# A binary-weight layer behind a two-way decaying scan: where the last batch's bias and x are added

## The chip, the cores and the metric

The kernel runs on one core of one Trainium2 chip. The metric is the time of one launch on the device in microseconds (us); lower is better. Engines go by the profile's names beside their own: PE is TensorE, DVE is VectorE, ACT is ScalarE, POOL is GpSimd, SP is SyncE, which only issues transfers here.

## The reference, cut to what matters

```python
def _bi_wkv(r, k, v, w, u, time_emb):          # r = x; k = v = fside; time_emb = cond
    tf = sigmoid(sum(time_emb, axis=-1))[:, None, None]
    decay = exp(-exp(w))[None, :] * (0.5 + 0.5 * tf[:, :, 0])
    ek = exp(minimum(k, 30.0)); ekv = ek * v
    # forward and backward scans over the tokens: a = a * decay + ekv_t, b = b * decay + ek_t
    nf, df = scan(ekv, ek); nb, db = scan(ekv, ek, reverse=True)
    euk = exp(minimum(u + k, 30.0))
    num = nf + nb - ekv + euk * v
    den = df + db - ek + euk
    return sigmoid(r) * (num / maximum(den, 1e-08)) * (0.8 + 0.2 * tf)

def binarize_weight(w):
    alpha = mean(abs(w), axis=1, keepdims=True)
    return where(w >= 0, 1.0, -1.0) * alpha

out = x + einsum('bsi,oi->bso', _bi_wkv(x, fside, fside, w, u, cond), binarize_weight(weight)) + bias
```

`x`, `fside` and `out` are [4, 1024, 1024] float32 (batch, token, channel), `weight` is [1024, 1024], `bias` is [1024].

## The kernel before, in words

Channels lie on partitions and tokens along the free dimension. The 4 batches of 8 channel blocks (128 channels, all 1024 tokens) make 32 steps, `for g in range(steps)`. The order of all instructions is written out by hand (`tc.manual_schedule()`); each engine works through its own list, and engines and transfers wait for each other by semaphores.

A step works at several blocks at once. SP loads block g + 2 of fside (`load_k`, tile `k_rows`) and of x (`load_gate`, tile `sg_rows`) and, in the first eight steps, 128 rows of the weight (`load_weight`, L237). TensorE transposes them. ScalarE takes the exponentials of the next block. VectorE runs the four scans of block g, forward (L366) and backward (L379), for `num` and for `den`. The backward scan begins from a value that ScalarE computes in `act_edge` (L372; `edge_num`, `edge_den`). For block g - 1, VectorE adds the own term to the denominator (`dve_denominator`, L389), and GpSimd issues a transfer that adds the own term `euk` into `num` (`dma_own_numerator`, L384). Then comes the division: GpSimd's `floor_den` (L396), ScalarE's logarithm (`act_log`, L404) and exponential (`act_reciprocal`, L411), GpSimd's `den_product` (L416) and `num_product` (L419), VectorE's gate with the sigmoid of x (`dve_newton_gate`, L423), GpSimd's `gated_product` (L428). For block g - 2 the result is split into two parts for TensorE, by ScalarE (`act_hi`, L433) and GpSimd (`lo_part`, L438). In steps 1 to 8 ScalarE also prepares the weight (`prepare_weight`, L247 and L254).

For batches 0 to 2 the product with the weight has output channels on partitions. ScalarE scales it and adds the bias (`act_scale`), TensorE turns it back, ScalarE copies it to a staging tile and SP stores it to `out`. Then x is added by an accumulating transfer from DRAM to DRAM, 256 rows (1 MB) at a time: `add_x` (L140), issued by GpSimd. The table `adds` gives the step for each; entry 32 means after the loop. In a step that has one, the logarithm is placed behind `act_edge` instead of ahead of it:

```python
            if g > 0 and not adds[g]:
                act_log(g - 1)
            ...
            act_edge(g, nums[g], "edge_num")
            if g > 0 and adds[g]:
                act_log(g - 1)
```

The last batch goes another way, with tokens on partitions, so that no turning back is needed. Its 8 groups of 128 tokens, in two halves of 512 channels each, are the "wide" products (`pe_wide_product`, L517). `leave_wide` (L534, L536) multiplies a sum in PSUM by `alpha_rows` and adds it to `x_rows[n]`, the 128 rows of x that `load_x_rows` (L479) has loaded. Group 6 (`begun`) is computed in two portions: its first five channel blocks in step 30, copied by ScalarE to `partials[0]`; its last three at the very end, in three pieces named `rest`. Products of groups 0 to 3 wait for the last two channel blocks; those of 4, 5 and 7 are done whole behind them. The `po` and `kT` PSUM buffers rotate among these sums. Before the change the bias of the last batch is loaded along rows into `bias_rows` (L496) and added to each `x_rows[n]` by `add_bias` (L831): by GpSimd for group 6, which also joins its partial sum there (L839, L840), by VectorE for the seven others. SP stores the rows (`store_rows`, L834).

Of the kernel before, what the change touches and what calls it, by code (L numbers as in the profile page):

```python
# [21 lines left out]
def kernel(  # L22
# [27 lines left out]
    nc = tc.nc  # L50
    P = 128
    B, T, C = x.shape
    TD = time_emb.shape[1]
    NT = T // P
    NC = C // P
# [6 lines left out]
    rows = ctx.enter_context(tc.tile_pool(name="rows", bufs=2))  # L62
# [3 lines left out]
    eu_pool = ctx.enter_context(tc.tile_pool(name="eu_pool", bufs=3))  # L66
# [47 lines left out]
    def group(q):  # L114
        b, r = divmod(q, NH * NC)
        h, oc = divmod(r, NC)
        return b, h, oc


    def pair_of(t, q):  # L120
        b, h, oc = group(q)
        return t[b, h * H : (h + 1) * H, oc * P : (oc + 2) * P].rearrange(
            "(n p) c -> p n c", p=P
        )
# [8 lines left out]

    def store(q):
        nc.sync.dma_start(out=pair_of(out, q), in_=x_pairs[q])

    def add_x(b, n):

        rows = slice(2 * n * P, 2 * (n + 1) * P)
        nc.gpsimd.dma_start(  # L140
            out=out[b, rows, :], in_=x[b, rows, :], accum_op=ALU.add, max_dma_last_dim=8192
        )
# [92 lines left out]
    def load_weight(oc):  # L235
        wr = resid.tile([P, C], F32, tag="x_res", name=f"w_rows_{oc}")
        nc.sync.dma_start(out=wr, in_=weight[oc * P : (oc + 1) * P, :])  # L237
        w_rows[oc] = wr
# [235 lines left out]
    x_rows = {}  # L474
    last = B - 1

    def load_x_rows(n, pool, tag):
        t = pool.tile([P, C], F32, tag=tag, name=f"x_rows_{n}")
        nc.sync.dma_start(out=t, in_=x[last, n * P : (n + 1) * P, :])  # L479
        x_rows[n] = t  # L480


# [11 lines left out]
    def load_along_rows(pool, tag, name, values):  # L494
        t = pool.tile([P, C], F32, tag=tag, name=name)
        nc.sync.dma_start(out=t, in_=values.unsqueeze(0).to_broadcast([P, C]))  # L496
        return t
# [35 lines left out]
    def leave_columns(ps, n, cols):  # L533
        nc.vector.tensor_mul(ps, ps, alpha_rows[:, cols])  # L534
        xs = x_rows[n][:, cols]
        nc.vector.tensor_add(xs, xs, ps)  # L536

    def leave_wide(n, part):
        leave_columns(wide[n, part], n, columns(part))


    begun = NT - 2
    partial_ps = {}
    partials = []
# [18 lines left out]
    steps = B * NC  # L563
# [25 lines left out]
    q, g = groups, 2 * NC  # L589
# [3 lines left out]
    q, g = 2 * groups, 3 * NC  # L593
# [6 lines left out]
    fill(g + 2, 0, pieces(range(q + 5, q + groups)))  # L600

    adds = {g: [] for g in range(steps + 1)}
    for b in range(B - 1):
        for n in range(NT // 2):
            adds[min((b + 2) * NC + 2 * n - 2, steps)].append((b, n))

# [5 lines left out]
    g = 3 * NC  # L616
# [3 lines left out]
    with tc.manual_schedule():  # L620
# [3 lines left out]
        for i, v in enumerate((u, bias)):  # L624
            nc.gpsimd.dma_start(
                out=ub_rows[i * NC : (i + 1) * NC, :],
                in_=v.rearrange("(n c) -> n c", c=P),
# [50 lines left out]
        for g in range(steps):  # L678
            b, cc = divmod(g, NC)
            final = g == steps - 1  # L680
            if g + 2 < steps:
                load_k(g + 2)
                for i in gate_loads[g]:
                    load_gate(i)
            else:
                load_x_rows(g + 2 - steps, rows, "k_rows")
                load_x_rows(g + 4 - steps, gate_rows, "sg_rows")
            if g < NC:
                load_weight(g)
            if final:  # L690
                alpha_rows = load_along_rows(den_pool, "den", "alpha_rows", alpha_dram)

            if g > 0:
                dve_denominator(g - 1)
                dma_own_numerator(g - 1)
            for i in adds[g]:
                add_x(*i)
            if final:
                done()
            scale()  # L700
            if final:
                act_partial(1)
            done()
            if g > 1:
                act_hi(g - 2, 0)
                act_hi(g - 2, 1)
            product(parts[g][0])
            if final:
                pe_wide_product(1, 1, range(NC - 3))
                pe_wide_product(2, 0, range(NC - 3))  # L710
            turn()
            if g > 0:
                floor_den(g - 1)
            if g > 0 and not adds[g]:
                act_log(g - 1)
            pool_clamp(g)
            if g > 1:
                lo_part(g - 2, 0)
                lo_part(g - 2, 1)
            product(late[g][:2])  # L720
            if late[g]:
                done()
            if g > 0:
                forward(g, nums[g])
# [3 lines that stand above are left out]
            if g > 0:  # L728
                act_reciprocal(g - 1)
                den_product(g - 1)  # L730
            if g > 0:
                dve_own_terms(g)
            scale()
            done()
            leave()
            if 1 <= g <= NC:
                prepare_weight(g - 1)
            if g == NC:
                out_scales()
            if not final:  # L740
                pe_transpose_k(g + 1)
                product(late[g][2:])
                act_exponentials(g + 1)
                act_own_exponentials(g + 1)
            scale()
            product(parts[g][1])
            turn()
            if final:
                for i in ((1, 0), (1, 1), (2, 0)):
                    pe_wide_product(*i, range(NC - 3, NC - 2))  # L750
                pe_wide_product(0, 0, range(NC - 2))
            backward(g, nums[g], "edge_num")
            if final:
                dma_own_numerator(g)
            if g > 0:
                num_product(g - 1)
            forward(g, dens[g])
            act_edge(g, dens[g], "edge_den")
            leave()
            done()  # L760
            scale()
            product(parts[g][2])
            if g == steps - 2:
                pe_partial(0)
            if g > 0:
                dve_newton_gate(g - 1)
            if g > 0 and not final:
                gated_product(g - 1)
            for i in gates[g]:
                act_gate(i)  # L770
            if gates[g]:
                log_exp_tables()
            pe_transpose_gate(g)
            if g == 3 * NC - 1:
                load_gate(g + 4)
            product(parts[g][3])
            turn()
            if g == steps - 2:
                leave()
                act_partial(0)  # L780
                pe_partial(1)
            if parts[g][4]:
                done()
            product(parts[g][4])
            if g == steps - 2:
                pe_wide_product(1, 0, range(NC - 3))
            leave()
            backward(g, dens[g], "edge_den")
            if not final:
                dve_numerator_terms(g + 1)  # L790
            if g == NC:
                store_alpha()
# [3 lines left out]
        g = steps - 1  # L796
# [27 lines left out]
            lo_part(g, h, nc.vector)  # L824
        for n in (5, 7):
            load_x_rows(n, eu_pool, "eu")

        bias_rows = load_along_rows(eu_pool, "eu", "bias_rows", bias)

        def add_bias(n, engine=nc.vector):  # L830
            engine.tensor_add(x_rows[n], x_rows[n], bias_rows)  # L831

        def store_rows(n, cols=slice(0, C)):
            nc.sync.dma_start(  # L834
                out=out[last, n * P : (n + 1) * P, cols], in_=x_rows[n][:, cols]
            )

        add_bias(begun, nc.gpsimd)
        nc.gpsimd.tensor_mul(partials[0], partials[0], alpha_rows)  # L839
        nc.gpsimd.tensor_add(x_rows[begun], x_rows[begun], partials[0])  # L840
        waiting = [(n, part) for n in range(4) for part in range(2)]
        for i in waiting:
            pe_wide_product(*i, range(NC - 2, NC))
        for i in waiting:
            leave_wide(*i)
        for n, part, biased in (
            (4, 0, (0,)), (4, 1, (1, 4)), (5, 0, (2, 3)), (5, 1, (5,)), (7, 0, (7,)), (7, 1, ())
        ):
            pe_wide_product(n, part, range(NC))

            for i in ((0, 1) if part else ()) if n == 5 else (part,):
                leave_wide(n, i)
            for i in biased:
                add_bias(i)
                if i != 7:
                    store_rows(i)
        store_rows(7)
        for cols in (slice(0, H), slice(H, 3 * H // 2), slice(3 * H // 2, C)):
            t = ps_o.tile([P, cols.stop - cols.start], F32, tag="po", name=f"rest_{cols.start}")
# [33 lines left out]
```

## Time and profile before

| what | value |
|---|---|
| device time, median of 3 runs | 489.73 us (489.09 to 491.17) |
| profiled execution | 489.64 us, span 487.9 us |
| mean granted TensorE clock | 0.898 |
| busy: VectorE, GpSimd, TensorE, ScalarE | 98%, 84%, 75%, 69% of the span |
| HBM read, written | 55.59 MB, 29.36 MB |
| the 12 `add_x` transfers | 1024 KB each, median 11.9 us from issue to landing |

The span runs from the first to the last instruction of the profiled execution; the rest of the device time lies around it. A line such as "start, us, engine line op out<-in" is one instruction or a run of like ones; brackets show the idle time of the engine ahead of it and what ended it. A landing is the time from a transfer's issue to its completion.

### The profile page before, as it was taken

To read this page: it belongs to the slowest core of one execution; us is meant where nothing else is said; L and a number is where in the kernel's file an instruction comes from. 1 tells how busy PE (TensorE), PEld (TensorE's weight loads), DVE (VectorE), ACT (ScalarE), POOL (GpSimd) and SP (SyncE) were. 2 spreads that over 40 slices of the span, in tenths; PEclk is the share of its full clock that TensorE was granted. 3 is DMA by queue.
4 is the path that set the end of the run, shared out by engine and by line. 5 is a ranking of instruction groups with operands and counts; after the bars stand their busy time and mean duration, and the time that the engine had idled before them with its cause. 6 is when DMAs were issued, how large, how long until landed. Compare 5 with 4: busy or idle time off the path is not lost.

```text
span 487.9 us, 5199 instructions
## 1 busy us (share of the span) xinstructions
PE 363.6 (75%) x1803; PEld 295.7 (61%) x1803; DVE 477.0 (98%) x330; ACT 337.3 (69%) x468; POOL 410.7 (84%) x279
## 2 busy tenths in 40 slices
PE   3434433344588877778899998965999998999995
PEld 2333332233466666656777777754887777887884
DVE  6999999999999999999999999999999999998997
ACT  4795968869595967869697879787866979734000
POOL 3379999999999999999999999999999999991240
PEclk9975566666699999999999999985999999999998
DMA  8865565556465555959787996889559697899743
GB/s 228 246 172 144 159 165 142 142 133 149 107 152 150 144 143 137 233 143 248 184 201 164 259 234 166 185 200 230 130 100 273 156 265 220 186 266 267 166 198 145
DMA packets 89761, 89.48 MB, mean 183 GB/s; under 512 B 2660, under 2 KB 80776, under 8 KB 88200
## 3 DMA queue, kind: packets, MB, share of 16 engines
q1 hardware_dynamic: 83320, 59.78, 40.9%
q0 software_dynamic: 6400, 29.37, 31.3%
q8 instruction: 14, 0.23, 0.2%
q14 instruction: 11, 0.09, 0.1%
q10 hardware_dynamic: 16, 0.00, 0.0%
HBM read 55.59 MB, written 29.36 MB: 174 GB/s over the span
## 4 chain that ended last, share of the span: by engine, by line
DVE 78%; PE 13%; issue 4%; ACT 3%; POOL 1%; DMA 0%; SPq 0%; DVEq 0%; ACTq 0%
DVE num L379 13%; DVE den L379 13%; DVE num L366 12%; DVE den L366 12%; DVE den L389 6%; DVE num L350 6%; DVE den L423 6%; PE wide L517 5%; DVE euk L356 3%; PE po L449 3%; DVE x_rows L831 2%; DVE x_rows L536 1%; DVE wide L534 1%; PE partial L517 1%; PE bank L517 1%
## 5 line engine op out<-in xcount | busy, mean ns | idle before, releaser
L449 PE MATMUL po<-gated,wT 128*128 128x512 f32 x768 | 199.4, 408 | 0.3 <-ACT staged L559 0.3
L449 PEld LDWEIGHTS po<-gated,wT 128*128 128x128 f32 x768 | 141.5, 192 | 30.5 <-ACT staged L559 0.7
L266 PE MATMUL kT<-ident,k_rows 128*128 128x128 f32 x248 | 42.1, 325 | 62.1 <-issue 43.2
L272 PE MATMUL sgT<-ident,sg_rows 128*128 128x128 f32 x256 | 43.2, 323 | 46.7 <-DVE den L423 41.4
L438 POOL TENSOR_TENSOR gated<-num,gated 128x512 fp32r<-128x512 f32 x60 | 75.8, 1283 | 2.4
L266 PEld LDWEIGHTS kT<-ident,k_rows 128*128 128x128 f32 x248 | 33.8, 167 | 69.7 <-issue 51.7
L379 DVE TENSOR_TENSOR_SCAN den<-bank,edge_den,den 128x1024 f32<-128x1024 f32 x32 | 74.8, 2338 | 0.4 <-ACT edge_den L372 0.4
L416 POOL TENSOR_TENSOR den<-den,eu 128x1024 f32<-128x1024 f32 x31 | 73.9, 2385 | 1.4 <-ACT eu L411 1.4
L379 DVE TENSOR_TENSOR_SCAN num<-bank,edge_num,num 128x1024 f32<-128x1024 f32 x32 | 74.8, 2336 | 0.0
L419 POOL TENSOR_TENSOR num<-num,eu 128x1024 f32<-128x1024 f32 x31 | 73.8, 2380 | 0.5 <-DMA num<-euk 0.5
L428 POOL TENSOR_TENSOR num<-den,num 128x1024 f32<-128x1024 f32 x30 | 71.8, 2394 | 2.8 <-DVE den L423 0.5
L366 DVE TENSOR_TENSOR_SCAN den<-bank,den 128x1024 f32<-128x1024 f32 x32 | 72.2, 2256 | 0.0
L366 DVE TENSOR_TENSOR_SCAN num<-bank,num 128x1024 f32<-128x1024 f32 x31 | 70.6, 2276 | 0.0
L272 PEld LDWEIGHTS sgT<-ident,sg_rows 128*128 128x128 f32 x256 | 35.0, 166 | 57.5 <-DVE den L423 30.2
L433 ACT CAST gated<-num 128x512 fp32r<-128x512 f32 x64 | 36.5, 619 | 28.6 <-POOL num L428 24.8
L396 POOL TENSOR_SCALAR den<-den,floor 128x1024 f32<-128x1024 f32 x31 | 37.1, 1196 | 19.8 <-DVE den L389 15.7
L404 ACT ACTIVATE eu<-den,gain 128x1024 f32<-128x1024 f32 (+1 forms) x33 | 36.9, 1121 | 24.3 <-POOL den L396 19.4
L517 PE MATMUL wide<-wT,gated 128*128 128x512 f32 x192 | 45.1, 392 | 0.0
L559 ACT COPY staged<-turned 128x512 f32<-128x512 f32 x48 | 27.5, 574 | 21.2 <-PE turned L469 21.2
L389 DVE SCALAR_TENSOR_TENSOR den<-eu,top,den 128x1024 f32<-128x1024 f32 (+1 forms) x33 | 41.5, 1259 | 0.0
L517 PEld LDWEIGHTS wide<-wT,gated 128*128 128x128 f32 x192 | 35.9, 188 | 8.2 <-ACT gate_of_last L810 0.4
L356 DVE SCALAR_TENSOR_TENSOR euk<-eu,top,kT 128x1024 f32<-128x1024 f32 x31 | 38.7, 1249 | 0.0
(100 smaller groups left out, 589.4 us busy)
## 6 DMA issues: line engine op xcount, KB each, us to landing
sg_rows<-in_x_dram SPq DMA_DIRECT2D x32, 512.0 KB, 6.3
num<-euk POOLq DMA_DIRECT2D x32, 512.0 KB, 5.8
k_rows<-in_fside_BxSxS_dram SPq DMA_DIRECT2D x31, 512.0 KB, 4.9
out_dram<-staged SPq DMA_DIRECT2D x24, 512.0 KB, 5.7
out_dram<-in_x_dram POOLq DMA_DIRECT2D x12, 1024.0 KB, 11.9
w_rows<-in_L_ffn_weight_dram SPq DMA_DIRECT2D x8, 512.0 KB, 5.9
x_rows<-in_x_dram SPq DMA_DIRECT2D x8, 512.0 KB, 7.7
out_dram<-x_rows SPq DMA_DIRECT2D x7, 512.0 KB, 2.6
```

The costliest lines, as they stand in the source:

```text
L266: nc.tensor.transpose(kT[:, s * P : (s + 1) * P], k_rows[g][:, s, :], ident)
L272: nc.tensor.transpose(t[:, s * P : (s + 1) * P], sg_rows[g][:, s, :], ident)
L356: nc.vector.scalar_tensor_tensor(euk, eus[g], top[:, b, cc : cc + 1], k_ps[g], ALU.min, ALU.mult)
L366: nc.vector.tensor_tensor_scan(t, decay_row(g), t, 0.0, ALU.mult, ALU.add)
L379: nc.vector.tensor_tensor_scan(back, decay_row(g), back, inits[g, which], ALU.mult, ALU.add)
L389: nc.vector.scalar_tensor_tensor(dens[g][:, ts], eus[g][:, ts], top[:, b, cc : cc + 1], dens[g][:, ts], ALU.min, ALU.add,)
L416: engine.tensor_mul(dens[g][:, ts], dens[g][:, ts], eus[g][:, ts])
L419: engine.tensor_mul(nums[g][:, ts], nums[g][:, ts], eus[g][:, ts])
L428: engine.tensor_mul(nums[g][:, ts], dens[g][:, ts], nums[g][:, ts])
L438: engine.tensor_sub(t[:, 1, :], nums[g][:, h * H : (h + 1) * H], t[:, 0, :].bitcast(F32))
L449: nc.tensor.matmul(prods[q], wT[:, cc, oc * P : (oc + 1) * P], gated[b, cc, h][:, i, :], start=(cc == 0 and i == 0), stop=(cc == NC - 1 an ...
L517: nc.tensor.matmul(t, gated[last, cc, h][:, i, s * P : (s + 1) * P], wT[:, cc, cols], start=(cc == ends[0] and i == 0), stop=(cc == ends[1 ...
```

## The change

Three things are changed. Rows of the last batch in `out` are filled with the bias by four transfers from SP (steps 2, 5, 7, 9; the bias row repeated 256 times), and x is added onto them by four `add_x` transfers from GpSimd (steps 6, 10, 12, 14). `load_x_rows` then reads `out` instead of x, so that x and bias arrive together. The `add_x` of the other batches move two steps later: those of batch 0 to steps 16 to 22, of batch 1 to 24 to 30, all four of batch 2 behind the loop, where three were before. At the end `bias_rows` and all `add_bias` go; VectorE joins group 6's partial sum behind the sums of group 4, in place of GpSimd; and rows are stored as soon as both their halves are done.

```diff
+    def begin_rows(n):
+        rows = slice(2 * n * P, 2 * (n + 1) * P)
+        nc.sync.dma_start(
+            out=out[B - 1, rows, :], in_=bias.unsqueeze(0).to_broadcast([2 * P, C])
+        )
...
     def load_x_rows(n, pool, tag):
         t = pool.tile([P, C], F32, tag=tag, name=f"x_rows_{n}")
-        nc.sync.dma_start(out=t, in_=x[last, n * P : (n + 1) * P, :])
+        nc.sync.dma_start(out=t, in_=out[last, n * P : (n + 1) * P, :])
...
     for b in range(B - 1):
         for n in range(NT // 2):
-            adds[min((b + 2) * NC + 2 * n - 2, steps)].append((b, n))
+            adds[min((b + 2) * NC + 2 * n, steps)].append((b, n))
+
+    begins = {g: n for n, g in enumerate((2, 5, 7, 9))}
+    for n, g in enumerate((6, 10, 12, 14)):
+        adds[g].append((last, n))
...
             if g < NC:
                 load_weight(g)
+            if g in begins:
+                begin_rows(begins[g])
...
-        bias_rows = load_along_rows(eu_pool, "eu", "bias_rows", bias)
-
-        def add_bias(n, engine=nc.vector):
-            engine.tensor_add(x_rows[n], x_rows[n], bias_rows)
...
-        add_bias(begun, nc.gpsimd)
-        nc.gpsimd.tensor_mul(partials[0], partials[0], alpha_rows)
-        nc.gpsimd.tensor_add(x_rows[begun], x_rows[begun], partials[0])
         waiting = [(n, part) for n in range(4) for part in range(2)]
         for i in waiting:
             pe_wide_product(*i, range(NC - 2, NC))
-        for i in waiting:
-            leave_wide(*i)
-        for n, part, biased in (
-            (4, 0, (0,)), (4, 1, (1, 4)), (5, 0, (2, 3)), (5, 1, (5,)), (7, 0, (7,)), (7, 1, ())
-        ):
+        for n, part in waiting:
+            leave_wide(n, part)
+            if part == 1:
+                store_rows(n)
+        for n, part in ((4, 0), (4, 1), (5, 0), (5, 1), (7, 0), (7, 1)):
             pe_wide_product(n, part, range(NC))
 
             for i in ((0, 1) if part else ()) if n == 5 else (part,):
                 leave_wide(n, i)
-            for i in biased:
-                add_bias(i)
-                if i != 7:
-                    store_rows(i)
+            if (n, part) == (4, 1):
+                nc.vector.tensor_mul(partials[0], partials[0], alpha_rows)
+                nc.vector.tensor_add(x_rows[begun], x_rows[begun], partials[0])
+            if part == 1 and n != 7:
+                store_rows(n)
         store_rows(7)
```

## The prediction, made before the result

> **What bounds the kernel now.** I read the page's busy times and its chain first.
>
> ```profile
> PE 363.6 (75%) x1803; PEld 295.7 (61%) x1803; DVE 477.0 (98%) x330; ACT 337.3 (69%) x468; POOL 410.7 (84%) x279
> ...
> DVE 78%; PE 13%; issue 4%; ACT 3%; POOL 1%; DMA 0%; SPq 0%; DVEq 0%; ACTq 0%
> ```
>
> VectorE is busy almost all the time and carries the chain: 32 steps of 13.5 us. But 98% is an average, and what the change takes off VectorE lies in the last 37 us only. So I read the timeline of that stretch.
>
> ```profile
> 454.78 23.97 PE L517 MATMUL wide<-wT,gated 128*128 128x512 f32 x104
> ...
> 463.56 3.23 DVE L831 TENSOR_TENSOR x_rows<-x_rows,bias_rows 128x1024 f32<-128x1024 f32 x1
> ...
> 478.59 2.24 PE L517 MATMUL rest<-wT,gated 128*128 128x512 f32 x12
> ...
> 480.11 0.69 DVE L534 TENSOR_TENSOR wide<-wide,alpha_rows 128x512 f32<-128x512 f32 x1
> ```
>
> The columns are start, length, engine, line. To be seen: TensorE runs 104 wide products without a break to about 478.75, and VectorE takes the last sum, (7, 1), at 480.11. VectorE is only 1.4 us behind TensorE there, whatever it did before.
>
> **The end, term by term.** VectorE loses seven `add_bias`. By the starts of the instructions behind them they take 3.15 (463.56 to 466.71) + 5.44 (four from 468.04 to 473.48) + 1.14 + 1.15 = 10.9 us. It gains two operations of the same size and kind (1.15 each) for the partial sum: 2.3 us. Net 8.6 us less work. How much of it counts is set by TensorE, whose instructions stay the same, in the same order. I lay the new VectorE list against the product times (16 matmuls of 0.230 us each, 23.97/104; the first eight of the 104 finish group 3). The eight waiting sums leave from 451.3 to 462.2 as now. The products of group 4 end at about 460.3 and 464.0, and their sums (1.33 us each) leave by 465.4. The partial sum follows to 467.7. Group 5 leaves after its second product (471.4) by 474.1, (7, 0), done at 475.1, by 476.4, and (7, 1) starts when its product ends at 478.75, not at 480.11. Ahead of each of these VectorE idles, 0.5 + 3.7 + 1.0 + 2.3 = 7.5 us in all. Behind (7, 1) lie the same sums as now, 4.4 us to 484.5. The third `rest` product waits for (7, 1)'s PSUM buffer as now, moved by as much, and ends about 0.6 us before VectorE asks for it. I allow 0.1 us for the hand-over: **-1.2 us**, bounds -1.4 (all of the lag) and 0. The stores behind it (3.4 us from 484.5 to the end of the span) are the same, and the others only leave earlier.
>
> GpSimd's three operations at the end (8.1 us), behind the bias load, ended by 469.1, before the path needed them: taking them out gives nothing. A fourth x transfer is issued at the end instead of three. The three issued from 438.2 landed after at most 21.7 us, by about 461; four at the same pace end by 468, and nothing waits for them but the program's end: nothing.
>
> **The loop: three more x transfers** (steps 6, 10, 12; the one in step 14 and those up to 30 take places that transfers of other batches have now). GpSimd queues the issue between the own-term transfer (L384) and `floor_den` (L396), whose chain runs over ScalarE's logarithm to `den_product` (L416) and VectorE's gate, L423. A step without one, a step with one, and the only stall:
>
> ```profile
> 88.75 1.11 POOL L396 TENSOR_SCALAR den<-den,floor 128x1024 f32<-128x1024 f32 x1 [0.78 <-DVE den L389]
> ...
> 195.88 1.14 POOL L140 DMA_DIRECT2D out_dram<-in_x_dram  x1
> 196.79 1.40 POOL L396 TENSOR_SCALAR den<-den,floor 128x1024 f32<-128x1024 f32 x1
> ...
> 258.71 1.22 DVE L423 SCALAR_TENSOR_TENSOR den<-den,sgT 128x1024 f32<-128x1024 f32 x1 [0.15 <-POOL den L416]
> ```
>
> The 0.78 us gap takes the issue in. What is left is VectorE's L389 of the step after, 1.33 us at 208.83 where 1.27 is usual, and one stall of 0.15 among the nine transfers in the loop now. Three more: 3 x 0.06 + 0.15 = **+0.3 us**, bounds 0 and 3 x 0.2. The issue also waits for its fill, which left SP four steps or more before: nothing.
>
> The Trainium skill (SBUF — State Buffer, "Who interferes with whom") says that a VectorE instruction with two SBUF inputs and a GpSimd instruction that reads SBUF lock each other out for the whole instruction. The first `add_bias`, 3.23 us beside GpSimd's product against 1.23 alone, agrees; what the lock would make of the three transfers goes into the third rival.
>
> **Step 6 has a cost that the diff hides.** In a step with a transfer the code puts the logarithm (L404, now at 89.89) behind `act_edge` (90.95 to 91.23). Steps 10 and 12 look like 14, where this stalls nobody. In step 6 ScalarE also prepares weights:
>
> ```profile
> 91.13 1.14 ACT L411 ACTIVATE eu<-eu,ln_g 128x1024 f32<-128x1024 f32 x1
> ...
> 96.40 0.29 ACT L372 ACTIVATE edge_den<-den,edge 128x1 f32<-128x1 f32 x1
> 97.41 2.33 DVE L379 TENSOR_TENSOR_SCAN den<-bank,edge_den,den 128x1024 f32<-128x1024 f32 x1
> ```
>
> Between 91.13 and 96.40 ScalarE has no gap. The logarithm (1.17 us to the next start in step 14) moves in at 91.13, so `edge_den` starts at about 97.6 and ends at 97.9, and the scan waits 0.5 us: **+0.5 us**, bounds 0.3 and 0.7.
>
> **The fills**, four of 1 MB on SP's queue behind a step's loads (steps 2, 5, 7, 9). No row shows a copy of this kind. The nearest, with the us from issue to landing last:
>
> ```profile
> num<-euk POOLq DMA_DIRECT2D x32, 512.0 KB, 5.8
> ...
> out_dram<-x_rows SPq DMA_DIRECT2D x7, 512.0 KB, 2.6
> ...
> bias_rows<-in_L_ffn_bias_dram SPq DMA_DIRECT2D x1, 512.0 KB, 13.1
> ```
>
> Twice 2.6 us to twice 13.1 us (the same repeated row, but read while three x transfers ran): 5 to 26 us; I take 8, near the first, since the DMA engines are only half busy there (share 0.59 in 67.5 to 81 and in 94.5 to 108). What is queued behind on SP comes a step later: k rows issued at 80.50 are first transposed some 25 us after and land in 4.9; gate rows wait 18 us for their sigmoid and land in 6.3. Even 26 us fits, so SP's queue costs nothing, nor do the x loads that now read `out`, whose transfers ended long before. What could show is the sharing of engines with `num<-euk`: issued at 87.10, read by GpSimd at 95.84, 8.7 us of room against 5.8. **0 us**; the upper bound is the second rival.
>
> The Trainium skill (DMA: Bandwidth & Descriptors, "Anatomy of one DMA") puts a transfer at about 2.0 us plus bytes over 436 GB/s, an estimate of 4.4 us for one fill; by that the sum is the same, and no run shows one yet.
>
> **Sum.** The profiled execution took 489.64 us (span 487.9 and 1.7 around it), 0.09 under the median of 489.73. 489.64 - 1.2 + 0.3 + 0.5 + 0 = 489.2, as a median 489.3. That is a change of 0.1%. A measurement of this kernel can tell about 0.5%, 2.4 us, from no change.
>
> **Rivals.** First: VectorE's work comes off whole, 489.3 - 8.6 + 1.2 = 481.9. For it: VectorE has hardly a gap from 451 to 484. Against: TensorE's unbroken row to 478.75, which would have to end before 471. Chance 0.04.
>
> Second, slower: the fills of steps 2, 5 and 7 hold back the `num<-euk` beside them. It decides once that lands more than 8.7 us after its issue; GpSimd then starts `num_product` late, has 0.8 us of gap to catch up, and VectorE's gate in the next step waits. At the longest 512 KB landing of the queue rows above, 13.1, each costs 13.1 - 8.7 - 0.8 = 3.6 us, three 11: 500. For it: GpSimd waits 0.5 us for this transfer once already. Against: its landings stay under 9.8 even beside x transfers and stores. Chance 0.08, most of it at 492 to 496.
>
> Third, slower: each new x transfer pushes a GpSimd instruction onto a VectorE one with two SBUF inputs, and VectorE is shut out for 2.0 us, as in the 3.23 us row: 489.3 + 3 x 2.0 = 495.3. Against: the nine transfers in the loop show 0.06 to 0.21. Chance 0.03.
>
> That the change doesn't do what it says I leave out: in the new order of instructions VectorE has seven additions fewer and two operations more, and nothing else of it moves.
>
> **How the numbers follow.** The forecast has 0.85. Its bounds are 488.3 (-1.4, nothing given back) and 491.1 (no gain, +1.3), nearly all within 0.5%. Faster gets the first rival and 0.01 of the forecast's edge, 0.05; slower the other two and 0.02 of it, 0.13; 0.82 stays the same. I stretch the range to 487.8 and 491.9 for the scatter of single runs (489.09 to 491.17 shown); it leaves out the rivals, 0.15.
>
> **What would show it.** In the new profile: (7, 1)'s sum starting at about 478.8 plus what the loop gave back, with idle time on VectorE put down to PE wide; step 6's scan waiting about 0.5 us for ACT `edge_den`; L389 at 1.33 after steps 6, 10 and 12; `num<-euk` still landing in about 6 us and the fills in about 8. It is wrong if VectorE shows no idle time behind TensorE at the end, or if GpSimd waits for `num<-euk`.

## The result and the profile after

The changed kernel took 488.21 us (median of 20 runs, 487.97 to 489.95), the kernel before 489.33 us on the same chip (20 runs, 488.14 to 491.22): a ratio of 0.9975, interval 0.9965 to 0.9984. That is 1.1 us less: the interval leaves out 1, so the gain is real, but it lies within the 0.5% that the prediction called no change. It is also 1.1 us under the forecast of 489.3, and 0.1 us under the 488.3 that the prediction's terms gave as their lower bound; it falls into the range of 487.8 to 491.9, which was stretched for the scatter of single runs. The profiled execution took 488.17 us, its span 486.4 us.

The page's busy times and its chain, as shown of before:

```profile
PE 364.9 (75%) x1803; PEld 297.1 (61%) x1803; DVE 468.9 (96%) x325; ACT 337.4 (69%) x468; POOL 406.2 (84%) x280
...
DVE 76%; PE 17%; issue 3%; ACT 3%; DMA 0%; SPq 0%; DVEq 0%; ACTq 0%
```

VectorE lost 8.1 us of work, and the time 1.5 us. TensorE's share of the chain rose from 13% to 17%: what VectorE no longer does at the end it spends waiting. The timeline of the end (start, length, engine, line; L523 was L517, L540 was L534) shows where:

```profile
454.84 23.97 PE L523 MATMUL wide<-wT,gated 128*128 128x512 f32 x104
...
464.20 0.70 DVE L540 TENSOR_TENSOR wide<-wide,alpha_rows 128x512 f32<-128x512 f32 x1 [0.49 <-PE wide L523]
...
471.52 0.70 DVE L540 TENSOR_TENSOR wide<-wide,alpha_rows 128x512 f32<-128x512 f32 x1 [3.50 <-PE wide L523]
...
475.19 0.70 DVE L540 TENSOR_TENSOR wide<-wide,alpha_rows 128x512 f32<-128x512 f32 x1 [0.79 <-PE wide L523]
...
478.85 0.70 DVE L540 TENSOR_TENSOR wide<-wide,alpha_rows 128x512 f32<-128x512 f32 x1 [2.25 <-PE wide L523]
```

The 104 products take the same 23.97 us, and VectorE now stands idle ahead of four sums, 0.49 + 3.50 + 0.79 + 2.25 = 7.0 us, each time for TensorE. (7, 1) starts at 478.85, right behind its product.

In the loop, take a step's length as the time from the start of the backward `den` scan of the step before to that of its own. From the first to the last of these scans the loop takes 419.66 us, against 419.52 before. It gives back 0.23 at step 6 (13.73 against 13.50) and 0.06 behind each of steps 10 and 12, and gains 0.20 at step 18 (13.55 against 13.75), which the prediction did not have. Step 6:

```profile
90.92 1.13 ACT L410 ACTIVATE eu<-den,gain 128x1024 f32<-128x1024 f32 x1
...
97.22 0.30 ACT L378 ACTIVATE edge_den<-den,edge 128x1 f32<-128x1 f32 x1
97.56 2.35 DVE L385 TENSOR_TENSOR_SCAN den<-bank,edge_den,den 128x1024 f32<-128x1024 f32 x1
```

The scan waits for ScalarE's `edge_den` as foretold, but for 0.2 us, not 0.5. Step 18 is read from three lines. The first is the x transfer's issue on GpSimd in before (L140). The second is the landing of the store that SP issued ahead of it, at 245.89. The third is the x transfer's issue after the change (L146).

```profile
250.54 0.86 POOL L140 DMA_DIRECT2D out_dram<-in_x_dram  x1 [0.22 <-issue]
```

```profile
out_dram<-staged SPq DMA_DIRECT2D x1, 512.0 KB, 4.0
```

```profile
250.30 1.16 POOL L146 DMA_DIRECT2D out_dram<-in_x_dram  x1
```

In before this transfer adds x to rows 512 to 767 of batch 0, and the last store to these rows is that one: issued at 245.89 with a landing of 4.0 us, it lets GpSimd start at 250.54. The row itself names no releaser for the 0.22 us; that it is the store is read from these times and borne out in experiment 1. With the x transfers two steps later, no store of the same rows is under way, and the wait is gone.

The queue rows of the two new kinds of transfer, and the landing of the `num<-euk` issued at 100.67, beside the third fill:

```profile
out_dram<-in_x_dram POOLq DMA_DIRECT2D x16, 1024.0 KB, 11.7
out_dram<-in_L_ffn_bias_dram SPq DMA_DIRECT2D x4, 1024.0 KB, 10.1
...
num<-euk POOLq DMA_DIRECT2D x1, 512.0 KB, 8.6
```

A fill lands in 10.1 us at the median. Beside the first three fills the `num<-euk` land in 7.8, 7.8 and 8.6 us, where the same three took 4.5 to 4.6 before. The point from which the prediction's second rival would decide was 8.7.

### The profile page after: what moved, and what is told of

It reads as the page before. It is cut to its first block, busy times and chain, and to the rows that moved or that the text cites. A ratio compares the mean times of both kernels' runs of the same rounds, so it can differ in the third digit from the quotient of the medians.

```text
span 486.4 us, 5204 instructions
## 1 busy us (share of the span) xinstructions
PE 364.9 (75%) x1803; PEld 297.1 (61%) x1803; DVE 468.9 (96%) x325; ACT 337.4 (69%) x468; POOL 406.2 (84%) x280
## 4 chain that ended last, share of the span: by engine, by line
DVE 76%; PE 17%; issue 3%; ACT 3%; DMA 0%; SPq 0%; DVEq 0%; ACTq 0%
DVE den L385 13%; DVE num L385 13%; DVE num L372 13%; DVE den L372 12%; PE wide L523 9%; DVE den L395 7%; DVE num L356 6%; DVE den L429 6%; DVE euk L362 3%; PE po L455 3%; PE partial L523 1%; PE wide_t L523 1%; PE bank L523 1%; PE sgT L278 1%; PE kT L272 1%
## 5 line engine op out<-in xcount | busy, mean ns | idle before, releaser
L523 PE MATMUL wide<-wT,gated 128*128 128x512 f32 x192 | 45.1, 392 | 0.0
L523 PEld LDWEIGHTS wide<-wT,gated 128*128 128x128 f32 x192 | 35.9, 188 | 8.2 <-ACT gate_of_last L821 0.4
## 6 DMA issues: line engine op xcount, KB each, us to landing
out_dram<-in_x_dram POOLq DMA_DIRECT2D x16, 1024.0 KB, 11.7
out_dram<-in_L_ffn_bias_dram SPq DMA_DIRECT2D x4, 1024.0 KB, 10.1
```

What stands on the lines that cost most here:

```text
L523: nc.tensor.matmul(t, gated[last, cc, h][:, i, s * P : (s + 1) * P], wT[:, cc, cols], start=(cc == ends[0] and i == 0), stop=(cc == ends[1 ...
```

## The experiments

Unless said otherwise, times are medians, and ratios are against the kernel before on the same chip with 95% intervals. Three groups of runs were made, with the kernel before at 489.79, 489.72 and 489.80 us.

**1. Which part does what.** Four kernels of the first group do parts of the change alone. The tail only (x is loaded as before, there are no fills, and the bias of the last batch is left out), as a diff against the changed kernel:

```diff
-        nc.sync.dma_start(out=t, in_=out[last, n * P : (n + 1) * P, :])
+        nc.sync.dma_start(out=t, in_=x[last, n * P : (n + 1) * P, :])
...
-            adds[min((b + 2) * NC + 2 * n, steps)].append((b, n))
-
-    begins = {g: n for n, g in enumerate((2, 5, 7, 9))}
-    for n, g in enumerate((6, 10, 12, 14)):
-        adds[g].append((last, n))
+            adds[min((b + 2) * NC + 2 * n - 2, steps)].append((b, n))
...
-            if g in begins:
-                begin_rows(begins[g])
```

> The end of the changed kernel alone: the loop, its x transfers and the x loads are those of the kernel before, there are no fills, and the last batch's bias is left out. Theory (TensorE's last products set the end as soon as VectorE has no backlog): -1.3 us against before, VectorE idle some 7 us at the end. Rival A (VectorE's removed work counts whole): -8.6 us. Rival B (the gain comes from the x transfers being two steps later): 0.

Measured: 487.67 us (12 runs), 0.9961 [0.9944, 0.9977]. The interval, 1.1 to 2.7 us less, leaves out both rivals, 8.6 and 0. The medians are 2.1 us apart, more than the lag of 1.4 us that the prediction saw at the end. Between the two profiled executions (487.61 and 489.64) the time from the start of the first wide sum to the end of the last gives 1.34 us of the difference, what follows the last sum 0.58 (2.80 against 3.38) and the start of the loop 0.19; why the last two are shorter was not tried.

The fills, the four new x transfers and the shift by two steps, with the tail of before (which writes over the filled rows), against the kernel before:

```diff
...
-            adds[min((b + 2) * NC + 2 * n - 2, steps)].append((b, n))
+            adds[min((b + 2) * NC + 2 * n, steps)].append((b, n))
+
+    begins = {g: n for n, g in enumerate((2, 5, 7, 9))}
+    for n, g in enumerate((6, 10, 12, 14)):
+        adds[g].append((last, n))
...
+            if g in begins:
+                begin_rows(begins[g])
```

> The loop of the changed kernel alone: four fills, four more x transfers and the others two steps later, with the end of the kernel before (x loaded from x, bias added at the end; what the fills wrote is overwritten). Theory: +0.1 to +0.2 us against before (step 6 +0.23, L389 by 0.06 three times, less a stall of 0.2 in step 18), as the profile of the changed kernel has it. Rival (the gain lies in the loop): -1.1 us. Rival (the fills hold back the own-term transfers): +1 us or more.

Measured: 489.13 us (12 runs), 0.9994 [0.9979, 1.0009]: no change that these runs can tell. The interval, 1.0 us less to 0.4 us more, holds the expected 0.1 to 0.2 and leaves out both rivals, the nearer one narrowly.

The shift alone, in the kernel before:

```diff
-            adds[min((b + 2) * NC + 2 * n - 2, steps)].append((b, n))
+            adds[min((b + 2) * NC + 2 * n, steps)].append((b, n))
```

> The kernel before with only the x transfers of batches 0 to 2 two steps later (four behind the loop). Theory: GpSimd no longer waits 0.22 us in step 18 for the last store of batch 0, whose rows it adds to, and VectorE's stall there goes: -0.2 us, and a few runs of before that are longer by 1 to 2 us are not explained by it. Rival (these waits make the scatter of the runs of before): -0.5 to -1 us, and the runs close together.

Measured: 488.74 us (12 runs), 0.9981 [0.9965, 0.9997]. The runs fall in two clumps, 488.07 to 488.78 and 489.44 to 490.38. The interval, 0.1 to 1.7 us less, narrowly leaves out no change, so moving the transfers is a gain by itself; it holds the expected 0.2 as well as the rival's 0.5 to 1, but the runs did not come close together. In the profile, step 18 has no wait left (13.57 us against 13.75), but the loop as a whole is hardly shorter, 419.48 us against 419.52, and 1.0 us of the profile's gain of 1.1 lies at the end, which experiment 3 explains. The fills and the x transfers of the last batch cost about 0.4 us by the medians (489.13 - 488.74; the intervals overlap, but the steps of the changed kernel give much the same, 0.23 + 0.06 + 0.06).

The kernel before without GpSimd's three operations at the end (group 6 is left without its bias and its partial sum):

```diff
-        add_bias(begun, nc.gpsimd)
-        nc.gpsimd.tensor_mul(partials[0], partials[0], alpha_rows)
-        nc.gpsimd.tensor_add(x_rows[begun], x_rows[begun], partials[0])
```

> The kernel before with all seven additions of the bias on VectorE, but without GpSimd's three operations at the end (group 6 gets neither its bias nor its partial sum). Theory: VectorE's lag of 1.4 us behind TensorE comes from the first addition of the bias, 3.15 us beside GpSimd's product instead of 1.15; without GpSimd beside it the lag goes: about -1.3 us, and the times of single runs lie closer together than those of before. Rival (the seven additions themselves make the lag): GpSimd was off the path, so 0 us, the sum of (7, 1) still starting 1.4 us behind TensorE.

Measured: 489.62 us (12 runs), 0.999 [0.9974, 1.0006]: by the time alone nothing. The profile says more. Step 18, and the landing of the store ahead of it (issued at 245.83):

```profile
251.20 0.86 POOL L140 DMA_DIRECT2D out_dram<-in_x_dram  x1 [0.95 <-DVE den L389]
...
259.38 1.22 DVE L423 SCALAR_TENSOR_TENSOR den<-den,sgT 128x1024 f32<-128x1024 f32 x1 [0.89 <-POOL den L416]
```

```profile
out_dram<-staged SPq DMA_DIRECT2D x1, 512.0 KB, 4.7
```

The loop is the same as in before, but here the store took 4.7 us in place of 4.0, GpSimd waited 0.95 us, and VectorE's gate at the end of GpSimd's chain 0.89 instead of 0.15. The row names `den` of L389, but that had ended at 250.68, half a microsecond earlier; the late one is the store. The issue follows its landing by 0.67 us here (245.83 + 4.7 to 251.20), by 0.65 in before (245.89 + 4.0 to 250.54), and by 0.60 and 0.64 in the two other profiles with the unshifted transfers. So the small stall of before's profile is one draw of something that varies over these four: 0.15, 0.89, 0.88 (group 5 cut, experiment 2), and none marked with the tail only, where the store took 3.9 us and step 18 still has 13.65 us against 13.55 in the changed kernel. The sum of (7, 1), with all seven additions still on VectorE:

```profile
479.53 0.70 DVE L534 TENSOR_TENSOR wide<-wide,alpha_rows 128x512 f32<-128x512 f32 x1 [0.60 <-PE wide L517]
```

The lag of 1.4 us is gone although VectorE's additions are not: from the first wide sum to the last the end takes 31.86 us, as in the changed kernel, against 33.20 in before. The 0.7 us lost at step 18 (0.89 - 0.15) hides half of this in the profiled execution. The single runs lie closer together than those of before (488.32 to 489.82, against 488.32 to 492.18), as expected. Their interval, 1.3 us less to 0.3 us more, hardly reaches the expected 1.3; where the rest of the gain went, one profile cannot settle.

**2. Is the end TensorE's?** Three kernels of the second group. Five more operations of 1.2 us on VectorE behind the join, in the changed kernel:

```diff
+                for _ in range(5):
+                    nc.vector.tensor_add(partials[0], partials[0], alpha_rows)
```

> The changed kernel with five more VectorE operations of 128x1024 (1.23 us each, about 6.0 us in all, on the partial sum's tile after its last use) behind the join of group 6's partial sum. Theory: VectorE idles 3.50 + 0.79 + 2.25 = 6.5 us behind that point, all for TensorE, so the time stays: 0 to +0.1 us. Rival (VectorE's work counts whole): +6 us.

Measured: 488.17 us (10 runs), 0.9969 [0.9957, 0.9981], the same as the changed kernel. 6.2 us more on VectorE vanish in the idle time, and the last wide sum still waits for TensorE:

```profile
468.32 6.26 DVE L859 TENSOR_TENSOR partial<-partial,alpha_rows 128x1024 f32<-128x1024 f32 x5
...
479.11 0.70 DVE L540 TENSOR_TENSOR wide<-wide,alpha_rows 128x512 f32<-128x512 f32 x1 [0.41 <-PE wide L523]
```

Half of the channel blocks of group 5 left out of its product, 16 matmuls or 3.7 us, once in the changed kernel and once in the one before:

```diff
-            pe_wide_product(n, part, range(NC))
+            if n == 5:
+                open_wide(n, part) if (n, part) not in wide else None
+                pe_wide_columns(wide[n, part], n, columns(part), range(NC // 2), (0, NC // 2 - 1))
+            else:
+                pe_wide_product(n, part, range(NC))
```

> The changed kernel with half of group 5's products left out (16 matmuls of 0.230 us, 3.7 us less on TensorE at the end). Theory: TensorE sets the end, VectorE has idle time enough to follow: -3.6 us against the changed kernel. Rival (VectorE sets the end): 0.

> The kernel before with the same half of group 5's products left out. Theory: VectorE works without a gap from 463.6 to the end there, so 3.7 us less on TensorE bring nothing: 0 us, at most -0.3. Rival (TensorE sets the end there too): -3.7 us.

Measured: 484.59 us (4 runs), 0.9896 [0.9872, 0.9919], for the changed kernel, 3.6 us less than the 488.2 of the uncut one; 488.66 us (10 runs), 0.9985 [0.9969, 1.0], for the one before, 1.1 us less. In the changed kernel TensorE's time at the end counts whole. In the one before it counts for less than a third; there the cut mostly lets TensorE wait for VectorE:

```profile
480.14 1.65 PE L517 MATMUL rest<-wT,gated 128*128 128x256 f32 x6 [1.62 <-DVE x_rows L536]
```

The 1.1 us were expected to be 0.3 at most. In this profile the first `add_bias` takes 1.22 us, not 3.23 (experiment 3), so VectorE has no lag to begin with: it takes (7, 1) at 478.68, where the uncut products would have ended at about 479.3 (an estimate: their start at 455.37 plus the 23.97 us of the uncut kernels). So TensorE's cut is worth some 0.7 us in this execution. The rest of the 1.1 is not explained.

**3. What made the lag.** In before's profile GpSimd works beside the first `add_bias` (shown in the prediction, 463.56, 3.23 us):

```profile
460.95 2.39 POOL L831 TENSOR_TENSOR x_rows<-x_rows,bias_rows 128x1024 f32<-128x1024 f32 x1 [19.91 <-DMA bias_rows<-in_L_ffn_bias_dram]
463.31 2.41 POOL L839 TENSOR_TENSOR partial<-partial,alpha_rows 128x1024 f32<-128x1024 f32 x1
465.79 3.27 POOL L840 TENSOR_TENSOR x_rows<-x_rows,partial 128x1024 f32<-128x1024 f32 x1
...
468.04 5.51 DVE L831 TENSOR_TENSOR x_rows<-x_rows,bias_rows 128x1024 f32<-128x1024 f32 x4
```

L839 ends at 465.72, and VectorE's addition of 1.2 us ends 1.1 us later, as if it had begun only then. The other profiles move the same pair:

| kernel | GpSimd's multiplication of L839 runs | first `add_bias` starts | takes | first wide sum to last |
|---|---|---|---|---|
| before | 463.31 to 465.72 | 463.56 | 3.23 us | 33.20 us |
| shift alone | 462.21 to 464.61 | 463.49 | 2.21 us | 32.18 us |
| loop part alone | 462.16 to 464.57 | 463.97 | 1.68 us | 31.93 us |
| before with group 5 cut | 461.87 to 464.27 | 464.15 | 1.22 us | 31.18 us (fewer products) |
| before without GpSimd's three | none | 464.30 | 1.22 us | 31.86 us |

There is a second collision, with L840 (465.79 to 469.06). The four additions from 468.04 take 5.51 us, and 5.50 or 5.51 in every profile with L840; without GpSimd's three they take 4.63:

```profile
466.77 4.63 DVE L831 TENSOR_TENSOR x_rows<-x_rows,bias_rows 128x1024 f32<-128x1024 f32 x4
```

In before the two collisions cost VectorE 2.01 + 0.88 = 2.9 us. Without them it stands idle for TensorE behind these additions, 0.81 us and then the 0.60 of experiment 1, 1.4 us together. What the collisions take beyond that, 1.5 us, is about the lag. The second one alone, 0.88 us, fits into the idle time, as the row of group 5 cut shows.

GpSimd begins when the bias load has landed, after 13.1 us in before, 12.0 with the shift alone and 11.0 with group 5 cut, so the lag hangs on the landing of one load. If the two waits, for the store and for GpSimd, are all that counts, the kernel before without them must be as fast as the changed one with all seven additions on VectorE (group 6 is again left without its bias and its partial sum):

```diff
-            adds[min((b + 2) * NC + 2 * n - 2, steps)].append((b, n))
+            adds[min((b + 2) * NC + 2 * n, steps)].append((b, n))
...
-        add_bias(begun, nc.gpsimd)
-        nc.gpsimd.tensor_mul(partials[0], partials[0], alpha_rows)
-        nc.gpsimd.tensor_add(x_rows[begun], x_rows[begun], partials[0])
```

> The kernel before with two causes of delay taken away at once and all seven additions of the bias still on VectorE: the x transfers of batches 0 to 2 two steps later (no wait for the last store of batch 0 in step 18), and GpSimd's three operations at the end left out (group 6 without its bias and partial sum). Theory: these two make all of the difference and the scatter, the seven additions themselves cost nothing: 487.5 to 487.8 us, runs within 0.6 us of each other. Rival (the seven additions cost something): about 488.7, as with the two-step shift alone.

Measured: 487.98 us (10 runs, 487.90 to 488.32), 0.9962 [0.9949, 0.9975]. The changed kernel, run beside it:

> The changed kernel once more, on the chip of the other three, as their reference: 488.0 to 488.4 us.

Measured: 488.22 us (12 runs, 488.00 to 488.40), 0.9964 [0.9951, 0.9977]. The first is no slower, and the kernel before scattered from 488.5 to 492.1 beside both. Its last wide sum waits for TensorE as the changed kernel's does:

```profile
478.58 0.70 DVE L534 TENSOR_TENSOR wide<-wide,alpha_rows 128x512 f32<-128x512 f32 x1 [0.59 <-PE wide L517]
```

So the seven additions on VectorE cost nothing. The extra time of the kernel before, and the scatter of its single runs, go when both waits go. One run of the changed kernel in the section on the result, 489.95 us, stands apart without either and is not explained.

**4. The fills.** Each fill issued twice, the second into a spare DRAM tensor:

```diff
+    spare = nc.dram_tensor("spare_rows", (NT * P, C), F32, kind="Internal").ap()
...
                 begin_rows(begins[g])
+                n = begins[g]
+                nc.sync.dma_start(
+                    out=spare[2 * n * P : 2 * (n + 1) * P, :],
+                    in_=bias.unsqueeze(0).to_broadcast([2 * P, C]),
+                )
```

> The changed kernel with every fill issued twice, the second time into a spare DRAM tensor. Theory: the fills are hidden, 0 to +0.2 us against the changed kernel. Rival (the fills hold back the own-term transfers or the loads): each further fill costs some tenths of a us to 3.6 us, +1 to +10 us.

Measured: 499.21 us (4 runs), 1.0186 [1.016, 1.0211], 11.0 us over the changed kernel. The theory had next to nothing here; it is the rival, and a little more than its 1 to 10 us. The profile shows how the second rival of the prediction comes about. The landing of the `num<-euk` issued at 32.36, and three lines of the timeline (L427 is `num_product`, L387 the backward scan, L431 VectorE's gate):

```profile
num<-euk POOLq DMA_DIRECT2D x1, 512.0 KB, 12.8
```

```profile
45.19 2.36 POOL L427 TENSOR_TENSOR num<-num,eu 128x1024 f32<-128x1024 f32 x1 [3.39 <-DMA num<-euk]
...
54.24 2.35 DVE L387 TENSOR_TENSOR_SCAN num<-bank,edge_num,num 128x1024 f32<-128x1024 f32 x1 [2.24 <-ACT edge_num L380]
...
103.98 1.22 DVE L431 SCALAR_TENSOR_TENSOR den<-den,sgT 128x1024 f32<-128x1024 f32 x1 [2.59 <-POOL den L424]
```

The three transfers beside fills of steps 2, 5 and 7 land in 12.8, 12.7 and 11.7 us, and GpSimd waits 3.4, 3.9 and 3.4 us for them (the second row names VectorE's `den` scan, which ended at the same moment). Steps 3, 6 and 8 grow by 3.2, 4.4 and 3.5 us against the changed kernel, 11.1 in all. The rival's rule (landing less 8.7 and 0.8) would give 3.3, 3.2 and 2.2, 8.7 in all. The size is near, but VectorE's wait is at the gate, as the rival had it, only in step 6. In steps 3 and 8 it is for ScalarE's `edge_num`, 2.24 and 2.23 us: the logarithm is placed ahead of it there and waits for GpSimd's late `floor_den`.

**5. Two versions that might be faster.** The logarithm of step 6 put back ahead of `act_edge`, in the changed kernel:

```diff
-            if g > 0 and not adds[g]:
+            if g > 0 and (not adds[g] or g == 6):
...
-            if g > 0 and adds[g]:
+            if g > 0 and adds[g] and g != 6:
```

> The changed kernel with the logarithm of step 6 put ahead of act_edge again, as in steps without an x transfer. Theory: edge_den no longer ends late, and VectorE's wait of 0.24 us in step 6 goes: -0.2 us against the changed kernel. Rival (the wait comes from the transfer on GpSimd, not from the order on ScalarE): 0.

Measured: 487.99 us (10 runs), 0.9962 [0.9951, 0.9973], 0.2 us under the changed kernel, as expected. The backward `den` scan of step 6 starts at 97.30 instead of 97.56, with the `num` scan ahead of it at 91.75 and 91.78:

```profile
97.30 2.36 DVE L385 TENSOR_TENSOR_SCAN den<-bank,edge_den,den 128x1024 f32<-128x1024 f32 x1
```

By the medians this beats both kernels, if by little; its interval and that of the changed kernel overlap, and it is the wait of step 6 that goes.

No fills: the transfers shifted, VectorE's tail as in the changed kernel, the bias loaded along rows as before and all eight `add_bias` on GpSimd (the diff, against the changed kernel, shows the last of these):

```diff
...
+        def add_bias(n):
+            nc.gpsimd.tensor_add(x_rows[n], x_rows[n], bias_rows)
...
+        for n in (4, begun, 5, 7):
+            add_bias(n)
         for n, part in waiting:
             leave_wide(n, part)
+        for n in range(4):
+            add_bias(n)
...
```

> A version that follows from the runs: the end of the changed kernel and the x transfers two steps later, but no fills and no x transfers for the last batch; GpSimd, idle at the end, adds the bias to all eight groups of rows (2.4 us each from about 461), while VectorE's sums there read only one operand from SBUF. Theory: as in the run of the end alone, 487.4 to 487.8 us, 0.5 us under the changed kernel. Rival (GpSimd's reads shut VectorE out of its sums too): VectorE's 0.69 us sums grow beside GpSimd's additions and the time is 489 or more.

Measured: 489.62 us (12 runs, 488.44 to 491.35), 0.9995 [0.9979, 1.0011]: no gain. The theory's 487.4 to 487.8 did not come; the time is the rival's, but its mechanism is not what the profile shows. The profiled execution, 488.62 us, is one of the quicker ones:

```profile
458.56 20.93 POOL L837 TENSOR_TENSOR x_rows<-x_rows,bias_rows 128x1024 f32<-128x1024 f32 x8 [16.74 <-DMA bias_rows<-in_L_ffn_bias_dram]
...
459.36 0.69 DVE L540 TENSOR_TENSOR wide<-wide,alpha_rows 128x512 f32<-128x512 f32 x1
...
466.89 3.25 DVE L860 TENSOR_TENSOR x_rows<-x_rows,partial 128x1024 f32<-128x1024 f32 x1
```

VectorE's sums, one operand of which is in PSUM, keep their 0.69 us beside GpSimd, and only the join's two operations are held up, to 1.39 and 3.25 us; they fit into the idle time behind them. VectorE ends at 483.10, as in the changed kernel when it ran beside. What this execution has more lies behind that: 3.4 us from there to the end of the span, against 3.1, and 2.1 to 2.2 us outside the span, in each of the 12 runs, against 1.7 to 1.8 in the changed kernel's. This profile does not show where the 490 and 491 of other runs come from. A later landing of the bias is a guess; it stays open.

## Why the prediction was right, and where it was not

It was right that the time hardly moves, and for the reason given: of 8 us off VectorE only its lag behind TensorE counts. Experiment 2 shows it in the changed kernel from both sides. That the number came out within the range was helped by the stretch of the range: the terms are off by 1.07 us together, every one of them to the same side. The sizes, from the two profiled executions:

| term | predicted, us | measured, us |
|---|---|---|
| end, from the first wide sum to the last | -1.2 | -1.34 (31.86 against 33.20) |
| more x transfers in the loop | +0.3 | +0.12 (0.06 behind steps 10 and 12; step 6's lies in the next row) |
| step 6, the logarithm | +0.5 | +0.23 |
| fills | 0 | 0 |
| the store's wait in step 18 | none | -0.20 |
| start of the loop; stores behind the last sum | 0 | -0.08; -0.2 |
| sum | -0.4 | -1.47 |

**The end** held in each of its parts: idle times of 0.49, 3.50, 0.79 and 2.25 against 0.5, 3.7, 1.0 and 2.3, and (7, 1) at its product's end. What the prediction took as given is the lag itself. It called GpSimd's three operations at the end worth nothing, since they ended before the path needed them. They had made the lag, by the two collisions of experiment 3: the 3.23 us row stood in the prediction's own fence, with the reason, and was used for a rival in the loop and not for the end. Where the collision is short the lag is too, as in the table of experiment 3, and this term would have been near zero.

**The loop's x transfers.** The term was 3 x 0.06 + one stall of 0.15, 0.3 in round numbers. The 0.06 held in steps 10 and 12. The stall was misread: it was taken as the price of a transfer, and it was the wait for a store of the same rows, which only step 18 has. So the change took it away, where the prediction added another; with the 0.06 counted twice in step 6, this is 0.4 us of the 1.07 by which the sum was off. The prediction said that nothing waits for the shifted transfers, and did not ask what they had waited for themselves.

**Step 6** was found by the order of the instructions, and sized too large: the logarithm began at 90.92, not at 91.13, and ScalarE's work from there to `edge_den` had 0.1 us less in it, so that it started at 97.22 and not at 97.6.

**The fills** cost nothing, but not by the margin given. The prediction's 8 us were 10.1, and the statement that `num<-euk` would still land in about 6 us was wrong beside fills: up to 8.6, with 8.7 as the limit. GpSimd was 0.1 us short of waiting by that mark, and VectorE, which the rival gave another 0.8 us, 0.9; doubling the fills brought the wait in, at 11.1 us where the rival's rule gives 8.7. A chance of 0.08 was low for that. For the fill the Trainium skill (DMA: Bandwidth & Descriptors, "Anatomy of one DMA") gave an estimate of 4.4 us, by a formula that the section states for transfers issued from GpSimd, while SP issues the fills; the measured 9.4 to 11.6 us decide.

**The other rivals** fell: VectorE's work did not come off whole, and the new transfers cost 0.06 us each, not the 2.0 of the third. Its mechanism was at work elsewhere: the Trainium skill (SBUF — State Buffer, "Who interferes with whom") has a VectorE instruction with two SBUF inputs shut out while GpSimd reads, and the 3.23, 2.21, 1.68 and 1.22 us of one and the same addition agree with it.

Medians say the same with less sharpness: the lag and the stall differ from run to run, so the gain is 1.1 us against one set of runs of before and 1.6 against another (489.80 - 488.22).

## What to carry to other kernels

When work comes off an engine, count only its lag behind the next engine, and then ask what made that lag: here it was not the work taken away but two collisions and a load's landing time. A kernel with a few transfers moved and without three GpSimd operations was as fast as the whole change; as it leaves out group 6's bias and partial sum, it shows the cause and is no replacement. A stall of 0.15 us in one profile can be one draw of something that ranges to 0.9; read what it waits for, by the landing of the transfers near it, before taking it as a price. A transfer that is hidden has a margin: compare its landing with its room, since up to 8.6 of 8.7 us the fills were free and at twice the amount they cost 11.

## What was not expected of the hardware

- A fill of 1 MB in DRAM from one repeated row takes 9.4 to 11.6 us from issue to landing, and an accumulating transfer on GpSimd's queue beside it goes from 4.5 to as much as 8.6 us; beside two fills, 12.8.
- SP's issue of a weight load can take longer with the change. The same load before and after, behind which the third fill is queued:

```profile
95.04 0.58 SPq L237 DMA_DIRECT2D w_rows<-in_L_ffn_weight_dram  x1
```

```profile
95.45 2.89 SPq L243 DMA_DIRECT2D w_rows<-in_L_ffn_weight_dram  x1
```

With doubled fills it is 3.7 to 4.3 us in three places. The cause was not tried. Each of these four issues ends within 0.2 us of the landing of a transfer on GpSimd's queue; the one shown ends at 98.34, and the x transfer issued at 87.60 lands after 10.9 us.
- Beside a GpSimd operation, VectorE's additions with two operands in SBUF lose up to 2.0 us each (3.23 against 1.22), and those with one in PSUM keep their 0.69 us.
